# Layer 0's source factors by way of memory, with smaller layer 0 steps, in a two-layer graph attention kernel

## The chip, the cores and the metric

The kernel runs on one core of one Trainium2 chip. The metric is the device time of one execution in microseconds; the median of three runs stands for the kernel. The lower the better.

## What is computed

Two graph layers run one after the other on 16 independent graphs ("blocks" of the batch) with 1024 nodes and 256 features each, all in float32. Cut to what matters here:

```python
# layer 0, four heads of 64 (the adjacency holds 0 or 1, so only edge type t = 0 occurs)
h = einsum('bnd,hde->bhne', x, W)
weight = e_src[:, :, :, None] + e_dst[:, :, None, :]     # h with a_src, h with a_dst
weight = leaky_relu(weight, 0.01)
weight = where(adj == 0, -1e9, weight)
out = relu(softmax(weight) @ h + bias) + h               # then a norm per head
x = layernorm(x + out)
...
# layer 1, eight heads of 32, queries = keys = values
normed = layer_norm(x)
scores = einsum('bhqd,bhkd->bhqk', qkv, qkv) * scale
attn = softmax(where(adj > 0, scores, -inf))
x = x + attn @ qkv
y = layer_norm(x)
x = layernorm(... + x + gelu(y @ W1 + b1) @ W2 + b2)
```

## The kernel before

**Layer 0's trick.** The exponential of the leaky rectifier of a sum is the larger of two products of factors. After a factor that cancels in the softmax, a weight is `max(source factor, destination factor) * mask`. The source factor is exp(0.99 e_src): one number for each node and head, wanted along the free dimension of a tile and equal on all 128 partitions. The destination factor `dinv` is one number for each partition. So one VectorE (DVE) instruction makes 128x512 weights: `p = max(cb, dinv) * mask` (`weights`, line 569), where `cb` holds the source factors of 512 nodes for two heads, spread over the partitions.

**How the source factors come about before.** `prepare` (line 481) goes through the eight groups of 128 nodes of a block, two at a time (`GB = 2`). For each it turns x and the adjacency on TensorE (`transpose_rows`, `turn_mask`), multiplies by `w0e` (264 columns: h, and the two logit terms), and ScalarE copies the four source logits of each node into `apart[g]`, 32 columns apart. `turn_sources` (line 538) transposes `apart` on TensorE and writes the exponential as rows into `esr`, a tile in on-chip memory, where head h lies at partition 32h. In `attention0` (line 551), `spread_factor` (line 558) spreads a row over the partitions: a matmul of a 32x128 matrix of ones in one row (`spread`) with 512 columns of `esr` for each of two heads, into two of the four PSUM banks `ps` that layer 1 uses as well, and two ScalarE copies into `cb`.

**Layer 0's attention.** 16 steps for each block: 2 halves of the queries (`n`), 4 heads, 2 parts of four key groups (`j4`). In a step TensorE does 32 matmuls (64 records, since a float32 matmul leaves two) of a 64-column tile each; in the profile they are `acc<-v,p`, a "bout" below. The weights of the next step are issued right after (`ps = weights(*steps[i + 1])`). After the last step of a head comes `residual0`; after every two heads `after0` (line 636) normalises, and after the fourth it also makes layer 1's input: normed, transposed into `nT`, with gains into `v1`.

**Layer 1.** `attention1` (line 720) has 32 steps a block: four logit matmuls of 32 rows each (`ps<-nT`, eight records) into four `ps` banks, four ScalarE exponentials of 128x512, two DVE mask products, and three steps later the products with the values (`po<-v,p`, `po<-p,v`, `po<-p,unit`). `mlp` (line 858) has 32 units of eight records (`ps<-yT,w_sb` with Gelu, and `po<-w_sb,hid`), and ends each group in `last_norm`, which stores the output by SyncE's queue (SP).

**What sets the order.** The program is unrolled. All instructions of TensorE (PE), ScalarE (ACT), DVE and GpSimd (POOL) stand in the order in which this Python code issues them. Layer 0 of block b+1 and layer 1 of block b are two generators; each `yield` gives a number of units of work and the things that the next part needs. The loop at line 1007 picks one at a time: layer 0 if its place (`done0 / WORK0`) is behind the course of `wanted()` (line 994), which rises with layer 1's place along `COURSE` (line 992), else layer 1; and the other one when the picked one's needs are later than the other's by more than 0.3 us in a model, within `SLACK`. The model is the class `Pace` (line 90): it holds for each engine when it is free, and for each tile when it was written and last read, from a cost for each instruction. Small chains (norms, transposes) are begun with `begin` and run by `advance` when the model says that they are ready. SP's DMA issues are not in that hand order.

```python
WORK0 = NB // GB * 3.25 + 2.0 + NB * H0 // 2 * 2.0
ATTN1 = 2.0 + 2.5 * (NH * NB * H1 // QUAD)
WORK1 = ATTN1 + NB // GB * (1.75 * FC / 2 + 3.5 * GB)
SLACK = 0.06
COURSE = [(0.0, 1.0), (ATTN1, 1.42), (WORK1 - 10.0, 2.0), (WORK1, 2.0)]
```

With the kernel's sizes WORK0 is 47, ATTN1 is 82 and WORK1 is 138: layer 0 of the next block is to be 42% done when layer 1's attention ends, and done ten units before the MLP's end. All helper calls go through one line, so the profile gives L61 for nearly everything; groups are told apart by their tiles.

Of the kernel before, what the change touches and what calls it, by code (L numbers as in the profile page):

```python
# [39 lines left out]
P = 128  # L40
# [49 lines left out]
class Pace:  # L90
# [20 lines left out]
    def through(self, tile):  # L111
        return max(self.written.get(tile, 0.0), self.read.get(tile, 0.0))

    def now(self):
        return self.free["tensor"]
# [55 lines left out]
def fast_path(  # L171
# [37 lines left out]
    Q = 32  # L209
    TILE = 64  # L210
    PAIR = 2
    GB = 2
# [12 lines left out]
    ]  # L225
    small = ring("small", 3)
    ps_s = ring("ps_s", 4, space=PSUM)
    ps_a = ring("ps_a", 1, space=PSUM)
# [10 lines left out]
    nc.vector.tensor_copy(identb, ident)  # L239

    spread = const.tile([P, P], F32, name="spread")
    nc.vector.memset(spread, 0.0)
    for h in range(H0):
        nc.vector.memset(spread[h * Q : h * Q + 1, :], 1.0)

# [18 lines left out]
    for c in range(DC):  # L264
        for h in range(H0):
            nc.scalar.dma_start(w0e[:, c, h * HO : (h + 1) * HO], w0[h, c * P : (c + 1) * P, :])

    apart = [const.tile([P, H0, Q], F32, name=f"apart{g}") for g in range(GB)]
    for t in apart:
        nc.vector.memset(t, 0.0)  # L270
    terms = ((a_src, nc.sync, w0e[:, :, D + H0 : D + 2 * H0]), (a_dst, nc.scalar, w0e[:, :, D : D + H0]))
# [208 lines left out]

    def prepare(b, hb, esr, v0, dinv, mask):

# [17 lines left out]

        turning, scaling = [], []
        for k in range(0, NB, GB):
            i = b * (NB // GB) + k // GB
            load_blocks(i + 1)
            xk = x_blocks.pop(i)
            xT = one.tile([P, DC, GB * P], F32, name="xT")
            transpose_rows(xT, xk)
            yield 0.45, bank0_ready
            turn_mask(k)
            yield 0.5, bank0_ready, xT  # L510
            if k % BPH == 0:

                finish_norms(b - 1, k // BPH)
                hb.append(one.tile([P, BPH, D], F32, name=f"hb{k // BPH}"))
            for g in range(GB):
                if g == 0:

                    for chain in turning:
                        complete(chain)
                ph, _ = bank0([P, D + 2 * H0])  # L520
                for c in range(DC):
                    nc.tensor.matmul(ph, xT[:, c, g * P : (g + 1) * P], w0e[:, c, :], start=c == 0, stop=c == DC - 1)
                nc.scalar.copy(apart[g][:, :, 0], ph[:, D + H0 : D + 2 * H0])
                nc.scalar.activation(v0[:, k + g, :, HO], ph[:, D : D + H0], AF.Exp)
                nc.scalar.activation(dinv[:, k + g, :], ph[:, D : D + H0], AF.Exp, scale=-0.99)
                scaling.append(values0(v0[:, k + g, :, :], ph))
                begin(scaling[-1], "vector", ph)
                nc.scalar.copy(hb[-1][:, (k + g) % BPH, :], ph[:, 0:D])
                yield 0.9, bank0_ready
                if g == 0:  # L530
                    turn_mask(k + 1)
                    yield 0.5, bank0_ready, xT
            turning.append(turn_sources(esr[:, k * P : (k + GB) * P]))
            begin(turning[-1], "tensor", bank0_ready, *apart)
        for chain in turning + scaling:
            complete(chain)

    def turn_sources(dst):
        es, _ = bank0([P, GB, P])
        for g in range(GB):  # L540
            nc.tensor.transpose(es[:, g, :], apart[g].rearrange("p h q -> p (h q)"), ident)
        nc.scalar.activation(dst, es.rearrange("p g q -> p (g q)"), AF.Exp, scale=0.99)
        yield from ()

# [5 lines left out]

    def attention0(b, hb, v0, esr, dinv, factors, mask, rinv):

        groups = [(n, pair) for n in range(NH) for pair in range(H0 // PAIR)]
        steps = [(n, hd, j4) for n in range(NH) for hd in range(H0) for j4 in range(0, NB, 4)]

        def spread_factor(n, pair):

            cb = two.tile([P, PAIR, HALF], F32, name="cb")  # L560
            pbs = [ps_s.tile([P, HALF], F32, name="ps") for _ in range(PAIR)]
            for e in range(PAIR):
                q = slice((pair * PAIR + e) * Q, (pair * PAIR + e + 1) * Q)
                nc.tensor.matmul(pbs[e], spread[q, :], esr[q, n * HALF : (n + 1) * HALF], start=True, stop=True)
            for e in range(PAIR):
                nc.scalar.copy(cb[:, e, :], pbs[e])
            return cb

        def weights(n, hd, j4):
            ps = []  # L570
            cb = cbs[n, hd // PAIR]
            for j2 in (j4, j4 + 2):
                p = four.tile([P, 2, HALF], F32, name="p0")
                for i in range(2):
                    nc.vector.scalar_tensor_tensor(
                        p[:, i, :],
                        cb[:, hd % PAIR, :],
                        dinv[:, j2 + i, hd : hd + 1],
                        mask[n][:, j2 + i, :],
                        op0=OP.max,  # L580
                        op1=OP.mult,
                    )
                ps.append(p)
            return ps

        def products(ps, hd, j4, av):
            for i in range(4):
                for q in range(BPH):
                    for at in range(0, P, TILE):
                        nc.tensor.matmul(  # L590
                            av[at : at + TILE, q, :],
                            ps[i // 2][:, i % 2, q * P + at : q * P + at + TILE],
                            v0[:, j4 + i, hd, :],
                            start=j4 + i == 0 and q == 0,
                            stop=j4 + i == NB - 1 and q == BPH - 1,
                        )

        cbs = {groups[0]: spread_factor(*groups[0])}
        yield 1.0,
        nc.vector.tensor_copy(factors, v0[:, :, :, HO])  # L600
        ps = weights(*steps[0])
        yield 1.0, bank0_ready, *ps
        for i, (n, hd, j4) in enumerate(steps):
            if j4 == 0:
                av, bank = bank0([P, BPH, HO + 1])
                bank["busy"] = True
            products(ps, hd, j4, av)
            advance()
            if i + 1 < len(steps):
                ps = weights(*steps[i + 1])  # L610
            if j4 == 0 and i + 3 < len(steps) and hd % PAIR == PAIR - 1:
                g = steps[i + 3][0], steps[i + 3][1] // PAIR
                cbs[g] = spread_factor(*g)
            if j4 == NB - 4:
                h = hb[n][:, :, hd * HO : (hd + 1) * HO]
# [5 lines left out]
                if hd % PAIR == PAIR - 1:  # L621
                    norms[b, n, hd] = after0(b, n, hd, hb[n])
                    begin(norms[b, n, hd], "vector", done(residual), hb[n])
            yield (2.0, *ps, *([bank0_ready] if j4 == NB - 4 else []))

# [94 lines left out]
    def attention1(half, mask, rinv, half_done):  # L720
# [8 lines left out]
        def exponentials(n, quad, jb):  # L729
            keys = slice(jb % BPH * P, (jb % BPH + 1) * P)  # L730
            of_keys, of_queries = half(jb // BPH)[2], half(n)[2]
            tiles = [ps_s.tile([P, HALF], F32, name="ps") for _ in range(QUAD)]
            for e in range(QUAD):
                q = slice(e * HD, (e + 1) * HD)
                nc.tensor.matmul(tiles[e], of_keys[q, quad, keys], of_queries[q, quad, :], start=True, stop=True)
            ps = []
            for e in range(0, QUAD, PAIR):
                p = eight.tile([P, PAIR, HALF], F32, name="p")
                for i in range(PAIR):
                    nc.scalar.activation(p[:, i, :], tiles[e + i], AF.Exp, scale=SCALE1)  # L740
                ps.append(p)
            return ps
# [198 lines left out]
    def layer0():  # L941
        for b in range(B):
# [5 lines left out]
            hb = []  # L948
            esr = one.tile([P, N], F32, name="esr")
            dinv = two.tile([P, NB, H0], F32, name="dinv")  # L950
            v0 = one.tile([P, NB, H0, HO + 1], F32, name="v0")
            mask = [two.tile([P, NB, HALF], U8, name=f"mask{n}") for n in range(NH)]
            yield from prepare(b, hb, esr, v0, dinv, mask)
            handed[b] = seen, rinv1, mask
            yield from attention0(b, hb, v0, esr, dinv, factors, mask, rinv0)
        place[0][:] = B, 0.0
# [30 lines left out]

    WORK0 = NB // GB * 3.25 + 2.0 + NB * H0 // 2 * 2.0
    ATTN1 = 2.0 + 2.5 * (NH * NB * H1 // QUAD)
    WORK1 = ATTN1 + NB // GB * (1.75 * FC / 2 + 3.5 * GB)  # L990
    SLACK = 0.06
    COURSE = [(0.0, 1.0), (ATTN1, 1.42), (WORK1 - 10.0, 2.0), (WORK1, 2.0)]

# [477 lines left out]
```

## Time and profile before

| what | value |
|---|---|
| median of 3 runs | 3573.72 us (3570.82 to 3583.27) |
| the profiled execution | 3564.78 us |
| its span, first to last instruction | 3563.0 us |
| PE matmul busy | 3443.4 us, 97% |
| DVE busy | 2989.8 us, 84% |
| ACT busy | 2010.2 us, 56% |
| mean granted TensorE clock | 0.983 |
| DMA | 97.51 MB in 77809 packets |

Times in the profile are microseconds from the first instruction, if not marked ns. A group's row gives the tiles as out<-in, the shapes, the count, then busy time, the mean ns of one, and the engine's idle time just before these instructions with what ended it. Matmul ends are modelled and matmuls overlap, so the distance from the start of one run of matmuls to the start of the next says more than their length: a matmul that waits may count as busy.

### The profile page before, as it was taken

How to read it: one execution, taken by the hardware profiler on the slowest of the kernel's cores; microseconds unless marked ns; L12 is line 12 of the kernel's file. 1: busy time of each engine (PE TensorE's matmuls, PEld its weight loads, DVE VectorE, ACT ScalarE, POOL GpSimd, SP SyncE). 2: the span in 40 equal slices, each digit the busy share in tenths (PEclk: the TensorE clock that was granted, in tenths of full speed). 3: DMA queues.
4: the chain of work that ended last, by engine and by line, in shares of the span. 5: the costliest groups of instructions: out<-in, count | busy, mean ns of one | idle time of the engine just before them, and what ended most of it. 6: DMA issues, size and time to landing. Idle time of an engine off the chain costs nothing.

```text
span 3563.0 us, 141472 instructions
## 1 busy us (share of the span) xinstructions
PE 3443.4 (97%) x64417; PEld 2329.2 (65%) x64417; DVE 2989.8 (84%) x5267; ACT 2010.2 (56%) x4320; POOL 413.7 (12%) x424
## 2 busy tenths in 40 slices
PE   6799999999999999999999999999999999999998
PEld 4458576675856658576585766757567585765846
DVE  5888898988888888898888979888798888988883
ACT  2564746547375563845647466474654737556373
POOL 0102011010110101011020110101101011010100
PEclk9899999999999999999999999999999999999999
DMA  4111101011020110201111010110201102010000
GB/s 107 32 20 34 30 14 41 12 34 30 16 45 9 37 24 17 47 12 35 21 30 33 13 39 15 34 30 14 41 13 33 30 16 45 9 37 9 16 6 14
DMA packets 77809, 97.51 MB, mean 27 GB/s; under 512 B 9104, under 2 KB 60048, under 8 KB 77200
## 3 DMA queue, kind: packets, MB, share of 16 engines
q0 software_dynamic: 18432, 33.56, 6.4%
q1 hardware_dynamic: 57184, 53.76, 5.0%
q8 instruction: 506, 8.29, 1.0%
q10 hardware_dynamic: 1584, 1.05, 0.1%
q14 instruction: 103, 0.84, 0.1%
HBM read 105.13 MB, written 16.78 MB: 34 GB/s over the span
## 4 chain that ended last, share of the span: by engine, by line
PE 91%; ACT 5%; DVE 2%; issue 1%; DMA 0%; POOL 0%; ACTq 0%; POOLq 0%; DVEq 0%
PE po L61 36%; PE ps L61 34%; PE acc L61 21%; ACT p L61 2%; DVE p L61 1%; ACT sq L61 1%; ACT mask L61 1%; ACT xT L61 0%; ACT z L61 0%; DMA w0e<-in_L_gnn_W_dram 0%; DVE hb L61 0%; ACT cb L61 0%; ACT hb L61 0%; POOL r L61 0%; DVE z L61 0%
## 5 line engine op out<-in xcount | busy, mean ns | idle before, releaser
L61 ACT ACTIVATE p<-ps 128x512 f32<-128x512 f32 x2048 | 1061.0, 616 | 417.3 <-PE ps L61 417.3
L61 DVE TENSOR_TENSOR p<-p,mask 128x1024 f32<-128x1024 f32 x1024 | 1188.9, 1217 | 27.0 <-ACT p L61 26.8
L61 PE MATMUL ps<-nT 32*128 32x512 f32 x4096 | 794.6, 651 | 12.3 <-ACT cb L61 9.8
L61 DVE SCALAR_TENSOR_TENSOR p<-cb,dinv,mask 128x512 f32<-128x512 f32 x1024 | 698.9, 743 | 23.3 <-ACT cb L61 23.3
L61 PEld LDWEIGHTS po<-v,p 128*32 128x32 f32 x32768 | 398.6, 110 | 317.0 <-issue 264.8
L61 ACT ACTIVATE hid<-ps,b_sb 128x256 f32<-128x256 f32 x512 | 242.5, 474 | 639.6 <-PE ps L61 639.6
L61 PE MATMUL acc<-v,p 128*64 128x65 f32 x16384 | 547.6, 225 | 18.3 <-DVE p L61 16.3
L61 PEld LDWEIGHTS acc<-v,p 128*64 128x64 f32 x16384 | 507.9, 139 | 83.6 <-issue 38.8
L61 PE MATMUL po<-p,v 128*32 128x512 f32 x2048 | 553.5, 615 | 0.0
L61 PE MATMUL po<-p,unit 128*32 128x512 f32 x2048 | 553.1, 615 | 0.0
L61 PE MATMUL ps<-yT,w_sb 128*128 128x256 f32 x2048 | 478.4, 383 | 0.0
L61 PE MATMUL po<-w_sb,hid 128*128 128x256 f32 x2048 | 474.6, 384 | 0.0
L61 PEld LDWEIGHTS po<-w_sb,hid 128*128 128x128 f32 x2048 | 381.7, 190 | 64.8 <-issue 11.4
L61 PEld LDWEIGHTS ps<-yT,w_sb 128*128 128x128 f32 x2048 | 380.3, 190 | 62.9 <-issue 11.4
L61 PEld LDWEIGHTS ps<-nT 32*128 32x128 f32 x4096 | 286.2, 186 | 166.2 <-ACT p L61 56.8
L61 PE MATMUL po<-v,p 128*32 128x33 f32 x32768 | 390.5, 198 | 4.4 <-issue 4.4
L61 PEld LDWEIGHTS po<-p,v 128*32 128x32 f32 x2048 | 78.7, 109 | 340.0 <-issue 210.8
L61 POOL TENSOR_TENSOR r<-v,mhalf 128x1 f32<-128x1 f32 (+1 forms) x192 | 152.8, 801 | 842.0 <-DVE v L61 493.0
L61 DVE TENSOR_TENSOR z<-acc,bias_r 128x256 f32<-128x256 f32 x128 | 54.1, 423 | 200.0 <-ACT hb L61 200.0
L61 POOL TENSOR_TENSOR r<-v1s,mhalf 128x4 f32<-128x4 f32 x32 | 61.7, 1927 | 1092.9 <-DVE v1s L61 1092.9
L61 POOL DMA_DIRECT2D ak<-in_adj_dram x128 | 69.7, 545 | 976.9 <-PE acc L61 963.1
L61 PE MATMUL acc<-w0e,xT 128*128 128x264 f32 x512 | 149.3, 415 | 20.0 <-issue 10.4
(109 smaller groups left out, 2909.4 us busy)
## 6 DMA issues: line engine op xcount, KB each, us to landing
ak<-in_adj_dram POOLq DMA_DIRECT2D x128, 256.0 KB, 3.9
xk<-in_x_dram SPq DMA_DIRECT2D x64, 256.0 KB, 2.8
xl<-in_x_dram SPq DMA_DIRECT2D x32, 512.0 KB, 3.9
out_dram<-z SPq DMA_DIRECT2D x128, 128.0 KB, 1.7
w_sb<-in_L_gnn_W_dram SPq DMA_DIRECT2D x2, 1024.0 KB, 6.7
v<-in_L_gnn_a_src_dram SPq DMA_DIRECT2D x2, 320.0 KB, 4.4
v<-in_L_gnn_a_dst_dram ACTq DMA_DIRECT2D x1, 320.0 KB, 6.5
xl<-in_L_gnn_a_dst_dram ACTq DMA_DIRECT2D x1, 320.0 KB, 7.8
```

The lines of the kernel that those rows point to most:

```text
L61: return method(*args, **kwargs)
```

## The change

There are four parts.

1. The source factors are no longer turned on TensorE. ScalarE writes exp(0.99 e_src) straight from the PSUM bank into a small tile `es` (128 nodes by four heads). A transfer on SP stores each `es[:, g, :]` with its two dimensions exchanged into `esr`, now a tile of four rows by 1024 in the chip's large memory with two buffers. `spread_factor` is now one transfer on SP, which reads two rows of 512 and writes them to all 128 partitions of `cb` (source stride 0 over partitions). The tiles `spread` and `apart`, `turn_sources`, the spreading matmuls and the copies to `cb` are gone. The first two `cb` of a block are loaded when half of `prepare` is done; the others at key group 2 of the second head of a pair, two pairs ahead.
2. A step of layer 0's attention has two key groups instead of four (32 steps of one unit instead of 16 of two units), and weights are issued three steps ahead (`AHEAD = 3`).
3. `Pace.together`: the model takes the four logit banks of a layer 1 step as free together, when the last one is, and as written together.
4. The course: 1.38 instead of 1.42, and layer 0 done 14 units before the MLP's end instead of ten. WORK0 keeps its value.

```diff
+    def together(self, tiles):
+        names = [t.tensor.name for t in tiles]
+        for times in (self.read, self.written):
+            times.update(dict.fromkeys(names, max(times.get(name, 0.0) for name in names)))
...
+    AHEAD = 3
...
+    memory = ctx.enter_context(tc.tile_pool(name="memory", bufs=2, space=bass.MemoryType.DRAM))
...
-                    for chain in turning:
-                        complete(chain)
...
-                nc.scalar.copy(apart[g][:, :, 0], ph[:, D + H0 : D + 2 * H0])
+                if g == 0:
+                    es = small.tile([P, GB, H0], F32, name="es")
+                nc.scalar.activation(es[:, g, :], ph[:, D + H0 : D + 2 * H0], AF.Exp, scale=0.99)
...
-            turning.append(turn_sources(esr[:, k * P : (k + GB) * P]))
-            begin(turning[-1], "tensor", bank0_ready, *apart)
-        for chain in turning + scaling:
+            for g in range(GB):
+                at = (k + g) * P
+                nc.sync.dma_start(esr[:, at : at + P].rearrange("h p -> p h"), es[:, g, :])
+            if k + GB == BPH:
+                for at in ((0, 0), (0, 1)):
+                    cbs[at] = spread_factor(esr, *at)
+        for chain in scaling:
             complete(chain)
-
-    def turn_sources(dst):
-        es, _ = bank0([P, GB, P])
-        for g in range(GB):
-            nc.tensor.transpose(es[:, g, :], apart[g].rearrange("p h q -> p (h q)"), ident)
-        nc.scalar.activation(dst, es.rearrange("p g q -> p (g q)"), AF.Exp, scale=0.99)
-        yield from ()
...
+    def spread_factor(esr, n, pair):
+        cb = two.tile([P, PAIR, HALF], F32, name="cb")
+        rows = esr[pair * PAIR : (pair + 1) * PAIR, n * HALF : (n + 1) * HALF]
+        nc.sync.dma_start(cb, bass.AP(tensor=rows.tensor, offset=rows.offset, ap=[[0, P], [N, PAIR], [1, HALF]]))
+        return cb
...
-        steps = [(n, hd, j4) for n in range(NH) for hd in range(H0) for j4 in range(0, NB, 4)]
-
-        def spread_factor(n, pair):
-
-            cb = two.tile([P, PAIR, HALF], F32, name="cb")
-            pbs = [ps_s.tile([P, HALF], F32, name="ps") for _ in range(PAIR)]
-            for e in range(PAIR):
-                q = slice((pair * PAIR + e) * Q, (pair * PAIR + e + 1) * Q)
-                nc.tensor.matmul(pbs[e], spread[q, :], esr[q, n * HALF : (n + 1) * HALF], start=True, stop=True)
-            for e in range(PAIR):
-                nc.scalar.copy(cb[:, e, :], pbs[e])
-            return cb
+        steps = [(n, hd, j) for n in range(NH) for hd in range(H0) for j in range(0, NB, PAIR)]
...
-        cbs = {groups[0]: spread_factor(*groups[0])}
-        yield 1.0,
         nc.vector.tensor_copy(factors, v0[:, :, :, HO])
-        ps = weights(*steps[0])
-        yield 1.0, bank0_ready, *ps
-        for i, (n, hd, j4) in enumerate(steps):
+
+        ps = [weights(*step) for step in steps[:AHEAD]]
+        yield 1.0, bank0_ready, ps[0]
+        for i, (n, hd, j) in enumerate(steps):
...
-            products(ps, hd, j4, av)
+            products(ps.pop(0), hd, j, av)
             advance()
-            if i + 1 < len(steps):
-                ps = weights(*steps[i + 1])
-            if j4 == 0 and i + 3 < len(steps) and hd % PAIR == PAIR - 1:
-                g = steps[i + 3][0], steps[i + 3][1] // PAIR
-                cbs[g] = spread_factor(*g)
-            if j4 == NB - 4:
+            if i + AHEAD < len(steps):
+                ps.append(weights(*steps[i + AHEAD]))
+            if j == NB - PAIR * AHEAD and hd % PAIR == PAIR - 1 and (n, hd // PAIR) in groups[:-2]:
+
+                at = groups[groups.index((n, hd // PAIR)) + 2]
+                cbs[at] = spread_factor(esr, *at)
+            if j == NB - PAIR:
...
-            yield (2.0, *ps, *([bank0_ready] if j4 == NB - 4 else []))
+            yield (1.0, *ps[:1], *([bank0_ready] if j == NB - PAIR else []))
...
+            nc.together(tiles)
             for e in range(QUAD):
                 q = slice(e * HD, (e + 1) * HD)
                 nc.tensor.matmul(tiles[e], of_keys[q, quad, keys], of_queries[q, quad, :], start=True, stop=True)
+            nc.together(tiles)
...
-    COURSE = [(0.0, 1.0), (ATTN1, 1.42), (WORK1 - 10.0, 2.0), (WORK1, 2.0)]
+    COURSE = [(0.0, 1.0), (ATTN1, 1.38), (WORK1 - 14.0, 2.0), (WORK1, 2.0)]
```

## The prediction, made before the changed kernel was run

> **What bounds the kernel now.** I read the page first (busy time, chain), then the groups of instructions, then windows of one middle block, then TensorE's timeline.
>
> ```profile
> PE 3443.4 (97%) x64417; PEld 2329.2 (65%) x64417; DVE 2989.8 (84%) x5267; ACT 2010.2 (56%) x4320; POOL 413.7 (12%) x424
> PE 91%; ACT 5%; DVE 2%; issue 1%; DMA 0%; POOL 0%; ACTq 0%; POOLq 0%; DVEq 0%
> ```
>
> TensorE (PE) is busy 97% of the span and carries 91% of the chain that ended last: a PE microsecond taken away counts, unless a wait behind it takes its place. Blocks repeat every 217 to 218 us. I split one in two: layer 1's MLP (with most of layer 0's attention between) and layer 1's attention (with layer 0's preparation of the next block).
>
> ```profile
> core 0: us, PE busy (x) PEld busy (x) DVE busy (x) ACT busy (x) POOL busy (x), PEclk, DMA share, GB/s
> 1341.00:1425.00 84.00, 84.00 (x992) 71.77 (x992) 72.03 (x159) 30.46 (x61) 16.93 (x14) 1.00 0.06 17
> 1425.00:1559.60 134.60, 131.17 (x3041) 73.34 (x3041) 114.14 (x169) 95.08 (x209) 8.87 (x12) 0.97 0.17 32
> ```
>
> The MLP stage, 84.0 us, is dense on PE (84.00 busy, clock 1.00), DVE at 86%. The attention stage, 134.6 us, looks as busy, but there a waiting matmul stretches: in the timeline eight logit records `ps<-nT` need 1.07 us from start to next start, and many take 1.70 to 3.3.
>
> The rows the change removes:
>
> ```profile
> L61 PE MATMUL ps<-esr,spread 32*128 32x512 f32 x256 | 72.1, 640 | 0.0
> L61 ACT COPY cb<-ps 128x512 f32<-128x512 f32 x128 | 68.7, 589 | 152.0 <-PE ps L61 152.0
> L61 PE MATMUL acc<-ident,apart 128*128 128x128 f32 x128 | 25.5, 280 | 0.2 <-ACT apart L61 0.2
> L61 ACT ACTIVATE esr<-acc 128x256 f32<-128x256 f32 x64 | 25.2, 394 | 0.0
> L61 ACT COPY apart<-acc 128x4 f32<-128x4 f32 x128 | 24.0, 188 | 50.5 <-PE acc L61 50.5
> ```
>
> [...] So each new store is 512 four-byte pieces, and the row load queues behind it; no store of this shape is in the trace. [...]
>
> **The change, per block of 217 us.** TensorE's timeline, MLP stage (start, length; I take start to next start):
>
> ```profile
> 1382.10 2.09 PE L61 MATMUL acc<-v,p 128*64 128x65 f32 x64
> 1384.12 1.13 PE L61 MATMUL ps<-esr,spread 32*128 32x512 f32 x4
> 1385.17 1.13 PE L61 MATMUL po<-w_sb,hid 128*128 128x256 f32 x4
> ```
>
> 1. *Spread matmuls, MLP stage:* 1385.17 − 1384.12 = 1.06 us, twice a block: −2.1.
> 2. *Spread matmuls, attention stage:*
>
> ```profile
> 1512.62 0.38 PE L61 MATMUL acc<-ident,apart 128*128 128x128 f32 x2
> 1512.93 1.13 PE L61 MATMUL ps<-esr,spread 32*128 32x512 f32 x4
> 1513.89 2.44 PE L61 MATMUL ps<-nT 32*128 32x512 f32 x8
> ```
>
> One pair costs 0.96 (1513.89 − 1512.93); a second (1538.89) runs beside logits. −1.0. Behind them the logits need 2.37 and 3.34 (1538.89 to 1542.22) instead of 1.07: they share the four `ps` banks and ScalarE must first copy `cb` out. That is 3.6 us of stall. Some returns as the ordinary 1.70 form (0.63 each); bounds 1.8 and 3.6, I take −2.7.
>
> 3. *Source transposes:* 1512.93 − 1512.62 = 0.31, four a block: −1.2.
> 4. *ScalarE in the attention stage:* off go 8 × 0.19 (`apart`), 4 × 0.39 (`esr`), 4 × 0.59 (`cb`) = 5.4; on come 8 exponentials of 128x4 at the 0.21 of the `v<-acc` row = 1.7. ScalarE is 95 of 134.6 us busy, so most is off the path: bounds 0 and −2, I take −0.7.
> 5. *Transfers:* 8 stores of 2 KB, 4 loads of 512 KB a block, all on SP. Nearest for the store: the 1024-element `b_sb` load, 2.2 us to landing; `g_c` 6.0 is the upper end. Nearest for the load: `xl`, 512 KB, 3.9. Chained, 6 to 10 us. The first two rows are loaded half-way through the preparation, tens of us early; a later one is issued eight half-steps before its first use (about 26 us at 3.3 us for half-step and MLP unit). I take 0; upper bound +1. Queued behind on SP: `xk` loads, which two buffers keep a block pair ahead, and output stores, 1.7 us with three `z` buffers. The store waits for ScalarE's exponential, the row load for DVE's last read of its buffer: SP may stand some us, covered by the same buffers. Without that cover DVE would stop at `z`, the stall itself being the price. DVE's wait on `cb` (23.3 us, 16 times) goes, but in blocks with layer 1 beside it PE has other work: 0.
> 6. *Layer 0 parts of two blocks.* Now 64 records take 2.02. Counting records in 1363.90 to 1364.40 and to 1365.00 (24, 44) gives 0.030 us a record, 1.9 for 64: starting a bout costs 0.10 to 0.15. MLP records before a same-mode transpose take 0.87 for four (1388.73 to 1389.60), 3.48 for 16; between two bouts 16 take 3.65 (1393.44 to 1397.10): 0.17 for entering and leaving. So 0.27 to 0.32 per bout, I take 0.30. The MLP stage had 11 bouts, about one per two MLP units. With half-units and a course rising (2.0 − 1.38)/42 × 1.75 × 47 = 1.2 half-steps per MLP unit, nearly every unit is followed by one: some 27 half-steps in 23 bouts. 12 more × 0.30 = +3.6; bounds 7 × 0.27 = +1.9 (many doubled) and 16 × 0.32 = +5.1.
> 7. *Course 1.42 to 1.38:* about five half-steps move from attention into the MLP. They cost 0.03 × 32 = 0.96 there and free slightly less where they filled stalls, while smaller pieces fill more of them: bounds −0.5 and +1.2, I take +0.5.
> 8. *Layer 0 ends four units earlier (−14):*
>
> ```profile
> 1425.00:1447.00 22.00, 20.29 (x221) 10.58 (x220) 17.42 (x42) 17.64 (x42) 3.72 (x5) 0.84 0.30 73
> ```
>
> The attention stage starts with ScalarE at 17.64 of 22 us, because the last norm and its transposes of layer 0 fall there, and PE at clock 0.84 (22 × 0.16 = 3.5 us lost). Four earlier units could move that into the MLP; the first logits, without products beside them, stay bound by exponentials. Bounds 0 and −4, I take −1.0.
>
> 9. *Logits together in the model:* no instruction changes, the order sees the wait for four banks. Bounds 0 and −3, I take −0.8.
>
> Sum: −2.1 − 1.0 − 2.7 − 1.2 − 0.7 + 3.6 + 0.5 − 1.0 − 0.8 = −5.4 us. Fifteen blocks of layer 0 run beside layer 1: −81. Block 0 runs alone and waits for DVE; losing transpose and `cb` at its start gives about −1 (DVE waited 0.67 on `cb` there). Together −82. The profiled execution took 3564.8 (span 3563.0 and 1.8 around it): 3483. The median of the runs is 3573.7, 9 higher: **3492**.
>
> **Rivals.**
> - *The start of attention empties* (8 and 4 in full): −10 a block, 3573.7 − 150 = 3424. For it: ScalarE's load and the clock there. Against: four units are 7 us, and the norm's chain ends in forced steps anyway.
> - *Switches eat the gain:* every half-step its own bout (+5.1), only 1.0 of item 2's stall saved, nothing from 4, 8, 9: −2.1 − 1.0 − 1.0 − 1.2 + 5.1 + 0.5 = +0.3, about 3575. For it: the half-units. Against: the stall behind `cb` is plain.
> - *Slower: DVE becomes what the MLP stage waits for.* Layer 0's share there rises from 1.04 to 1.2 half-steps per MLP unit. DVE: 72 us less 44 × 0.68 (698.9 us busy over 1024 on the `p<-cb,dinv,mask` row) leaves 42 of other work; over 24 dense units 1.75, plus 1.2 × 1.37 = 3.4. PE: 1.74 + 1.2 × 0.96 + 0.30 = 3.2. From an average wait of 5.4/24 = 0.22 us per half-step it is slower; at 0.35 it costs 8.4, so +3.0 a block and 3619. Against: 42 spreads over the whole stage, and weights run three half-steps ahead.
> - *The transfers don't do it:* a row later than 26 us. Against: 6 to 10 us. Counted with the last.
>
> **Chances.** Forecast 0.63, its own range 3440 to 3555; empty start 0.17; eaten 0.08; DVE or late rows 0.12. Range 3410 to 3578: it leaves out the lower third of the empty start (0.06), the slower case (0.12) and an edge of the eaten one (0.02). What a measurement can tell is about 0.3%, 11 us: faster 0.80, same 0.08, slower 0.12.
>
> **What would show it.** No `spread` or `apart` rows; `ps<-nT` total below 794.6; about 23 MLP bouts of 32 records at 1.1 us; MLP stage some 87 us, attention stage some 125; PE busy down by some 80. Wrong if DVE's `p` ends PE's waits in the MLP stage, if bouts stay paired, or if DVE waits for a `cb` transfer.

## The result and the profile after

The changed kernel is slower by a quarter: median 4461.36 us of 4 runs (4444.25 to 4478.3) against 3575.71 us of 4 runs of the kernel before (3570.82 to 3583.27), a ratio of **1.2483 [1.2442, 1.2524]**. The forecast was 3492. The profiled execution took 4444.25 us, with a span of 4442.5, 879.5 above the 3563.0 of before. One run of a kernel below (rows_course) took 4648.44 us at a granted clock of 0.629, against 0.97 in its other three, and is left out of its figures.

The page's first lines and its chain, after:

```profile
span 4442.5 us, 140860 instructions
PE 3592.3 (81%) x64033; PEld 2364.6 (53%) x64033; DVE 2986.4 (67%) x5260; ACT 1920.9 (43%) x4128; POOL 431.5 (10%) x424
PE 74%; issue 17%; ACT 6%; DVE 2%; DMA 1%; another core or an unknown queue 0%; POOL 0%; ACTq 0%; POOLq 0%; DVEq 0%
```

The instructions went as planned: 384 matmuls fewer, DVE the same, ScalarE 89 us less. Yet TensorE carries 74% of the chain instead of 91%, and 17% of it, some 755 us, is "issue": an engine that waits for nothing that the profile shows. Next, the same two stages of a middle block as before, in the after profile's windows:

```profile
core 0: us, PE busy (x) PEld busy (x) DVE busy (x) ACT busy (x) POOL busy (x), PEclk, DMA share, GB/s
1705.10:1793.90 88.80, 88.80 (x1122) 75.45 (x1116) 75.97 (x169) 28.70 (x59) 18.13 (x14) 1.00 0.08 25
1793.90:1980.00 186.10, 136.83 (x2795) 71.12 (x2797) 109.72 (x158) 91.50 (x199) 8.82 (x12) 0.81 0.29 30
```

The MLP stage (84.0 before) is 88.8 us and full, near the 87 of the forecast. The attention stage went from 134.6 to 186.1 with fewer instructions on TensorE, DVE and ScalarE. TensorE stands for 49 us of it (186.10 − 136.83; before 3.4), and its clock fell from 0.97 to 0.81. Eight stores of `es` fall into this stage. One of them in the after profile's timeline (lines of other engines and runs left out):

```profile
243.72 16.85 SPq L61 DMA_DIRECT2D esr<-es  x2
...
244.93 4.62 DVE L61 TENSOR_TENSOR p<-p,mask 128x1024 f32<-128x1024 f32 x4
...
246.97 0.53 POOL L61 DMA_DIRECT2D ak<-in_adj_dram  x1 [7.56 <-PE acc L61]
...
248.62 0.61 PE L61 MATMUL po<-v,p 128*32 128x33 f32 x48
257.43 0.48 PE L61 MATMUL po<-v,p 128*32 128x33 f32 x16 [8.19 <-issue]
257.84 2.13 PE L61 MATMUL acc<-w0e,xT 128*128 128x264 f32 x4
```

A run of 64 equal products breaks off after 48. TensorE stands 8.19 us, waiting for nothing that the profile shows ("issue"), and goes on with the other 16, which read tiles of the same names. DVE had finished its last mask product (244.93 + 4.62) 7.9 us before TensorE went on. TensorE resumes 13.7 us after SP began on the first of the two stores. The waits of the whole profile (us in total, times, longest) put most of it at these products:

```profile
PEld po L61 <- issue: 1219.2, 1334, 11.7
PE po L61 <- issue: 672.5, 157, 11.5
```

Before, they were:

```profile
PEld po L61 <- issue: 487.7, 1166, 1.5
PE po L61 <- issue: 4.4, 8, 0.9
```

And what the forecast feared of the transfers did not come: DVE waited 3.5 us for `cb` in all, in the row of its weights:

```profile
L61 DVE SCALAR_TENSOR_TENSOR p<-cb,dinv,mask 128x512 f32<-128x512 f32 x1024 | 709.7, 743 | 3.5 <-DMA cb<-esr 3.5
```

### The profile page after: what moved, and what is told of

Read it like the earlier page. It is cut to its first block, busy times and chain, and to the rows that moved or that the text cites. A ratio compares the mean times of both kernels' runs of the same rounds, so it can differ in the third digit from the quotient of the medians.

```text
span 4442.5 us, 140860 instructions
## 1 busy us (share of the span) xinstructions
PE 3592.3 (81%) x64033; PEld 2364.6 (53%) x64033; DVE 2986.4 (67%) x5260; ACT 1920.9 (43%) x4128; POOL 431.5 (10%) x424
## 3 DMA queue, kind: packets, MB, share of 16 engines
q0 software_dynamic: 18432, 33.56, 12.5%
q8 instruction: 503, 8.24, 1.0%
## 4 chain that ended last, share of the span: by engine, by line
PE 74%; issue 17%; ACT 6%; DVE 2%; DMA 1%; another core or an unknown queue 0%; POOL 0%; ACTq 0%; POOLq 0%; DVEq 0%
PE po L61 30%; PE ps L61 26%; PE acc L61 18%; ACT p L61 2%; DVE p L61 1%; ACT mask L61 1%; ACT sq L61 1%; ACT o L61 1%; DMA esr<-es 1%; ACT z L61 0%; DMA w0e<-in_L_gnn_W_dram 0%; ACT hb L61 0%; DMA cb<-esr 0%; ACT oT L61 0%; DVE hb L61 0%
## 5 line engine op out<-in xcount | busy, mean ns | idle before, releaser
L61 PEld LDWEIGHTS po<-v,p 128*32 128x32 f32 x32768 | 451.2, 117 | 1029.8 <-issue 979.4
L61 PE MATMUL po<-v,p 128*32 128x33 f32 x32768 | 460.2, 205 | 661.5 <-issue 660.8
L61 PE MATMUL ps<-nT 32*128 32x512 f32 x4096 | 776.0, 745 | 23.8 <-issue 22.0
L61 PE MATMUL po<-p,v 128*32 128x512 f32 x2048 | 600.5, 662 | 11.6 <-issue 11.6
L61 PE MATMUL po<-p,unit 128*32 128x512 f32 x2048 | 599.8, 662 | 0.0
L61 PE MATMUL acc<-v,p 128*64 128x65 f32 x16384 | 575.5, 226 | 25.2 <-DVE p L61 19.9
L61 PEld LDWEIGHTS ps<-nT 32*128 32x128 f32 x4096 | 250.7, 213 | 135.8 <-issue 75.6
L61 ACT ACTIVATE mask<-acc,shift_c 128x1024 uint8<-128x1024 bf16 x128 | 144.3, 1127 | 354.7 <-PE acc L61 275.6
L61 POOL TENSOR_TENSOR r<-v,mhalf 128x1 f32<-128x1 f32 (+1 forms) x192 | 171.3, 900 | 660.3 <-DVE v L61 574.7
L61 DVE RECIPROCAL ranges<-po 128x8 f32<-128x8 f32 x64 | 13.3, 208 | 288.6 <-PE po L61 288.6
```

The source lines that it names most:

```text
L61: return method(*args, **kwargs)
```

## Which part costs it: three runs

My theory was that the 128 stores, each of 512 four-byte pieces that lie side by side in memory, stop TensorE, and that nobody's waiting for their data matters. The rival was the half steps with the new order. (Beside the queue of the stores, the page of after has a queue of kind `instruction`, q8, with 503 packets of 16 KB; more on it below.) The times below stand beside runs of the kernel before on the same chip, 3578.79 us for these three.

**stores_beside**: the kernel before, with the stores of the change added; nothing reads `aside`. (This and the later kernels with `aside` compute what the kernel before does, and additionally the unread tile.)

```diff
+        aside = memory.tile([H0, N], F32, name="aside")
...
+                if g == 0:
+                    es = small.tile([P, GB, H0], F32, name="es")
+                nc.scalar.activation(es[:, g, :], ph[:, D + H0 : D + 2 * H0], AF.Exp, scale=0.99)
...
+            for g in range(GB):
+                at = (k + g) * P
+                nc.sync.dma_start(aside[:, at : at + P].rearrange("h p -> p h"), es[:, g, :])
```

> The kernel before, with the change's 128 stores (512 pieces of 4 bytes each) added from a tile of their own into memory that nothing reads; ScalarE also makes the 128 small exponentials. No instruction waits for the data. Theory A (the stores hold up other transfers, among them the fetching of TensorE's instructions, some 7 us each): 3576 + 128 x 6.9 = about 4460 us, TensorE idle with 'issue' some 800 us. Rival B (the new order of the work costs the time) and rival C (the row loads into cb, or what waits for them): 3576 to 3610 us.

Measured: 4530.24 us, 951 more than before, 7.4 us a store. The waits of this kernel look like those of after:

```profile
PEld po L61 <- issue: 1156.8, 1305, 10.5
PE po L61 <- issue: 599.4, 151, 10.4
```

The stores alone give the whole loss. Nothing waits for them.

**rest_alone**: the change without its first part. Source factors as before (TensorE and `cb` copies), with half steps, weights three ahead, `together` and the new course.

```diff
+    AHEAD = 3
...
-        steps = [(n, hd, j4) for n in range(NH) for hd in range(H0) for j4 in range(0, NB, 4)]
+        steps = [(n, hd, j) for n in range(NH) for hd in range(H0) for j in range(0, NB, PAIR)]
...
+            nc.together(tiles)
...
+    COURSE = [(0.0, 1.0), (ATTN1, 1.38), (WORK1 - 14.0, 2.0), (WORK1, 2.0)]
```

> The kernel before with its own way to the source factors (transpose, spreading matmul, copies), but with steps of two key groups, weights three steps ahead, logits together in the model and the new course. Theory A: 3576 plus what the prediction's items 6 to 9 give, +3.6 +0.5 -1.0 -0.8 = +2.3 us a block, about 3610 us (3540 to 3650). Rival B: over 4300 us. Rival C: like A.

Measured: 3568.91 us, 0.9974 [0.9962, 0.9985]. Parts 2 to 4 cost nothing here; on the old path they even save 9 us.

**rows_store**: the changed kernel, but the factors are turned on TensorE as before and stored as rows: four pieces of 1 KB for every two node groups. The loads that spread `cb` stay.

```diff
-                nc.sync.dma_start(esr[:, at : at + P].rearrange("h p -> p h"), es[:, g, :])
...
+        for g in range(GB):
+            nc.tensor.transpose(es[:, g, :], apart[g].rearrange("p h q -> p (h q)"), ident)
+        row = small.tile([P, GB * P], F32, name="row")
+        nc.scalar.activation(row, es.rearrange("p g q -> p (g q)"), AF.Exp, scale=0.99)
+        nc.sync.dma_start(dst, row[0:P:Q, :])
```

> The changed kernel, but the source factors are turned on TensorE as before and stored as four runs of 1 KB instead of 1024 pieces of 4 bytes for two blocks; the 64 row loads into cb, the half steps, the model and the course are the changed kernel's. Theory A: the stall goes, and what the prediction forecast remains less the transposes that stay (1.2 + 0.5 us a block): about 3518 us (3430 to 3580). Rival B and rival C: over 4300 us.

Measured: 3543.46 us, 0.9899 [0.9882, 0.9915]. Between after and this kernel lie 4442.5 − 3543.9 = 898.6 us of span, 7.0 for each of the 128 stores. The 64 loads of 512 KB, with source stride 0 over the partitions, are no problem: DVE's idle time before the weights that read `cb` is 0.0 us here. So it is the stores, and their shape.

## What in the shape: four runs

Each is stores_beside with another layout of `aside`; the payload is always 2 KB.

**stores_spaced**: each four-byte piece in a 512-byte stretch of its own.

```diff
-        aside = memory.tile([H0, N], F32, name="aside")
+        aside = memory.tile([H0, N, P], F32, name="aside")
...
-                nc.sync.dma_start(aside[:, at : at + P].rearrange("h p -> p h"), es[:, g, :])
+                nc.sync.dma_start(aside[:, at : at + P, 0].rearrange("h p -> p h"), es[:, g, :])
```

> As stores_beside, the same number of 4-byte pieces, but every piece goes to 512 bytes of its own in memory instead of beside its neighbour. If pieces that share a stretch of memory must be written one after the other (A1): near 3600 us. If each small piece costs by itself wherever it goes (A2): 4400 to 4500 us as in stores_beside. Rivals B and C: 3576 to 3610 us.

**stores_64b** and **stores_4perline**: the same with `[H0, N, 16]` (64 bytes apart) and `[H0, N, 4]` (16 bytes apart).

> As stores_spaced, but the pieces lie 64 bytes apart instead of 512. If it is 64-byte lines that are shared in stores_beside: near 3590 us as in stores_spaced. If the shared stretch is longer, up to 512 bytes: clearly over 3700 us.

> As stores_64b with the 4-byte pieces 16 bytes apart, so four of them to 64 bytes; 512 pieces a store. If the pieces of one 64-byte line are written one after the other, a store lands in about a quarter to a third of the 12 to 14 us, 3 to 5 us, [...]: 3580 to 3650 us. If touching pieces are what matters, 3585 us and 2.2 us to landing; if a longer stretch is shared, over 3900 us.

**stores_16b**: no exchange of dimensions; 128 adjacent pieces of 16 bytes.

```diff
+        aside = memory.tile([N, H0], F32, name="aside")
...
+                nc.sync.dma_start(aside[at : at + P, :], es[:, g, :])
```

> The kernel before with 128 unread stores of the same 2 KB, as 128 adjacent pieces of 16 bytes (four heads of a node side by side). A quarter of the pieces; if the pieces of one shared stretch are written one after the other, a quarter of stores_beside's loss or less [...]: 3580 to 3800 us. If any store under 512 bytes a piece costs a fixed time: 4400 us.

| store | time, us | before on that chip | a store costs |
|---|---|---|---|
| 4 B pieces side by side | 4530.24 | 3578.79 | 7.4 |
| 4 B pieces, 16 B apart | 3586.9 | 3575.3 | 0.09 |
| 4 B pieces, 64 B apart | 3585.47 | 3567.15 | 0.14 |
| 4 B pieces, 512 B apart | 3588.43 | 3578.79 | 0.08 |
| 16 B pieces side by side | 3583.97 | 3567.15 | 0.13 |

Each of these kernels was run once. The 10 to 18 us that the last four lie above the kernel before are no more than that kernel's own spread (3556.91 to 3578.0 in its seven runs around 3567.15). The number of pieces is the same 512 in the first four rows: stores_beside and stores_spaced both have 145396 packets, 76688 of them under 512 bytes. That is 528 a store more than before ((145396 − 77809) / 128); in stores_16b, with 128 pieces, it is 144, so each piece is a packet and 16 more come with a store. The line of the page of stores_spaced:

```profile
DMA packets 145396, 97.80 MB, mean 27 GB/s; under 512 B 76688, under 2 KB 127632, under 8 KB 144784
```

So neither the count of pieces nor their size costs anything that matters; what costs is four-byte pieces side by side (distances between 4 and 16 bytes were not tried). The profile's DMA view has the time to landing of the other stores (last column, median us). For stores_spaced:

```profile
aside<-es SPq DMA_DIRECT2D x128, 2.0 KB, 2.5
```

for stores_64b:

```profile
aside<-es SPq DMA_DIRECT2D x128, 2.0 KB, 2.2
```

and for stores_16b:

```profile
aside<-es SPq DMA_DIRECT2D x128, 2.0 KB, 2.1
```

That is what the prediction had taken for the store (2.2). For the two other shapes the view gives no time, but the trace has increments of the stores' semaphores. With pieces 16 bytes apart all 16 increments of a store are recorded, and the last comes 4.5 us after the issue (median of 128 stores). With adjacent pieces only some are recorded, five in the median. The last of these comes 13.7 us after the issue in stores_beside and 12.9 in after (medians over the stores with no other within 13 us), so these are lower bounds.

The time to landing thus rises from 2.2 us over 4.5 to some 13 as one, four or 16 four-byte pieces share 64 bytes. The 4.5 lie in the 3 to 5 us that were expected for pieces of the same 64 bytes written one after the other. That neighbours wait for each other fits, but is not shown: in stores_16b four pieces share 64 bytes as well, and they land in 2.1 us. Small pieces at a distance cost this kernel nothing that can be told from its spread; only four-byte pieces right beside each other do.

## Why TensorE stands: two runs

TensorE reads nothing that the stores write. So I looked at what else the stores hold up. The queue of the adjacency loads on the page of before (packets, MB, share of 16 engines):

```profile
q0 software_dynamic: 18432, 33.56, 6.4%
```

and this queue and that of instructions on the page of after:

```profile
q0 software_dynamic: 18432, 33.56, 12.5%
...
q8 instruction: 503, 8.24, 1.0%
```

The adjacency loads move the 33.56 MB of before in packets that take 2.4 times as long together (12.5% of 4442.5 us against 6.4% of 3563.0): the stores do slow transfers that have nothing to do with them. The start of every packet is in the trace. In stores_beside 90 stores have no other within 13 us. Nine in ten of these have begun all their 512 pieces within 2.6 us of the issue. Then, from 3 to 10 us after the issue, 5.8 packets a microsecond begin, of all queues together, against 32 in the mean of the run; after 52 of the 90 stores it is at most one packet in these 7 us. In after it is so behind 52 of 91. So it is not the taking in of the pieces that lasts: behind an adjacent store nearly all of the core's transfers stand still.

As to q8, 8.24 MB in 503 packets is 16 KB a packet; TensorE's 64033 matmuls and as many weight loads, divided by 503, are 255 instructions a packet. With TensorE's own waits and branches counted in (128373 records in after), the packets keep step with 256 of its instructions: 91% of them begin within one half of a cycle of 256 in after and 96% in before, against 52 to 55% with a cycle of 255 or 257. With the kind of the queue, `instruction`, it fits that these packets bring TensorE's instructions. A theory is then that TensorE runs out of instructions ("issue" is 1% of the chain before and 17% after). How many it has in hand no run shows; the stops counted below come after some 250.

To see whether a store starves TensorE, I wanted stores where it uses instructions more slowly: in the MLP stage 1984 matmuls and loads in 84.0 us (24 a microsecond), against 6082 in 134.6 us (45) in the attention stage: a little over half the rate.

**stores_mlp**: the kernel before, with the stores in the MLP and a constant tile as their source.

```diff
+                if f % 4 == 0:
+                    at = (n * BPH + q + f // 4) * P
+                    nc.sync.dma_start(aside[:, at : at + P].rearrange("h p -> p h"), unit[:, 0:H0])
```

> As stores_beside (128 unread stores of 512 adjacent 4-byte pieces, eight a block), but issued in layer 1's MLP, where TensorE works through its instructions at less than half the rate of the attention stage. If TensorE starves of instructions behind a store (A), what it has in hand lasts about twice as long there and most of a store's time is covered: under 3576 + 128 x 3.5 = 4020 us, near 3700 to 3950. If it waits for data that the store holds up, or is stopped by the store itself (D): about as in stores_beside, 4300 to 4530 us.

Measured: 3696.18 us against 3567.15. This run did not test what it was made for. Its source is ready from the start, so nothing holds SP back, and SP issued the stores in one go at the beginning, where they only delayed the x loads behind them. SP's timeline of stores_mlp:

```profile
74.21 164.74 SPq L61 DMA_DIRECT2D aside<-unit  x103
```

and its longest wait of TensorE, most of the loss of 129 us in one place:

```profile
PE acc L61 <- ACT sq L61: 101.9, 1, 101.9
```

The other blocks last 217.5 us as before. What it tells is only that a chain of such stores holds up what is queued behind it on SP, by some 1.6 us each (164.74 / 103).

**stores_mlp2**: as stores_mlp, but each stored tile is a copy that ScalarE makes there.

```diff
+                if f % 4 == 0:
+                    at = (n * BPH + q + f // 4) * P
+                    es = small.tile([P, H0], F32, name="es")
+                    nc.scalar.copy(es, hid[f // 4][:, f % 4, 0:H0])
+                    nc.sync.dma_start(aside[:, at : at + P].rearrange("h p -> p h"), es)
```

> The kernel before, with 128 stores of 512 adjacent four-byte pieces that nothing reads, eight in each block's layer-1 MLP. This time the stored tile is a copy that ScalarE makes of four columns of `hid` right there, so SP can't issue a store before its place. In the attention stage such a store cost 7.4 us (stores_beside). There TensorE works through some 45 matmuls and weight loads a microsecond (6082 in 134.6 us), in the MLP stage through 24 (1984 in 84.0). Theory A, TensorE runs out of instructions because the store holds up the engines that bring them: at half the rate the instructions in hand last longer, so a store costs half as much or less, 1 to 4 us: 3700 to 4080 us, with TensorE's idle time put down to issue. Theory B, the store stops TensorE for a time of its own, whatever it executes: 7 to 7.5 us each: 4460 to 4540. Theory C, the store hurts only where something of the attention stage (the adjacency load on POOL's queue, the x loads) waits beside it: under 3620.

Measured: 3921.13 us against 3583.5, a single run of each, 2.6 us a store: inside what theory A gave, far from the others. Two stores in this kernel's timeline, lines of TensorE's matmuls and of SP, and one of DVE:

```profile
1524.65 0.36 SPq L61 DMA_DIRECT2D aside<-es  x1
1525.55 2.09 PE L61 MATMUL acc<-v,p 128*64 128x65 f32 x64
...
1527.57 3.72 PE L61 MATMUL ps<-yT,w_sb 128*128 128x256 f32 x16
1531.19 0.55 SPq L61 DMA_DIRECT2D aside<-es  x1
1531.22 1.73 PE L61 MATMUL acc<-v,p 128*64 128x65 f32 x51
...
1532.52 2.73 DVE L61 SCALAR_TENSOR_TENSOR p<-cb,dinv,mask 128x512 f32<-128x512 f32 x4
...
1538.70 0.96 PE L61 MATMUL acc<-v,p 128*64 128x65 f32 x13 [5.75 <-issue]
```

After the first store TensorE works on for more than 8 us, through a bout, 16 slow records and most of another bout, then it breaks off after 51 records of 64. DVE does not: three of its four `p` start while TensorE stands.

Counted in the trace, for stores with no other within 13 us, is what TensorE executed between the store's issue and the longest stop that begins in the 16 us behind it:

| kernel | such stores | with a stop over 2 us | instructions until the stop, median (10% to 90%) | issue of the store to resumption, us, median |
|---|---|---|---|---|
| stores_beside | 90 | 88 | 248 (204 to 332) | 12.2 |
| after | 91 | 91 | 253 (211 to 297) | 11.4 |
| stores_mlp2 | 15 | 3 | 248 to 256 (all three) | 14.9 to 16.1 (all three) |

In the attention stage TensorE executes some 250 instructions in the 5.4 to 5.5 us (medians) behind the issue, stops, and goes on when the store is about landed. Behind the last store of each MLP in stores_mlp2 the same 250 instructions need 13 us, and by then little of the store is left. In twelve of the fifteen cases TensorE doesn't stop for 2 us. In three it stands 2.1 to 3.2 us, from 12.8 us or later, which the profile puts down to ScalarE's exponentials. So a store costs TensorE about the time that is left until it lands when some 250 instructions have gone by. That much the runs show.

That TensorE comes to the end of the last packet's instructions is not shown, and two things in the trace speak against it in this plain form. First, it would then always stop at the same place of the 256. Counted from the program's start in stores_beside, 92% of q8's packets begin within one half of the 256 instructions; of the 88 stops no half holds more than 51 (in after, 55 of 91). Second, a packet of q8 takes 1.48 us in the mean in after (1.08 before; the longest 9.8), and in 85 of the 88 stops in stores_beside none is under way in the last microsecond before TensorE goes on. Whether TensorE waits for instructions whose packet is already over, or for something else that goes with each of its instructions (the profiler's own records, say), no run tells: none without the profiler is on record. A halt of the whole core it is not, as DVE's line above shows. What it is that holds TensorE stays open.

## The other terms of the sum: four runs

With the stores out of the way, the rest of the forecast can be checked. Their kernel before ran at 3567.15 us for the first, 3575.3 for the others.

**rows_only**: the kernel before with rows_store's path for the factors, and old steps, old model and old course: items 1 and 2 alone.

> The kernel before with the source factors by way of memory in 1 KB rows as in rows_store, but with steps of four key groups, the old model and the old course. The prediction's items 1 and 2 alone (-2.1 -1.0 -2.7 = -5.8 us a block) would give 3576 - 87 = 3489 us. From the two runs at hand (rest_alone 0.9974, rows_store 0.9899 of before) the parts add up if this is 0.9925, 3552 us: then items 1 and 2 were two to three times too large.

Measured: 3493.6 us, **0.9783 [0.975, 0.9816]**. The logit row shows where: 766.0 us, with the spread records and the stall behind them gone (794.6 before):

```profile
L61 PE MATMUL ps<-nT 32*128 32x512 f32 x4096 | 766.0, 660 | 1.5 <-ACT p L61 1.3
```

**hops**: rows_only without the transposes: items 3 and 4 as well. The factors go to memory in 16-byte pieces, each half comes back as four rows, goes out again as rows of 2 KB, and is spread from there.

```diff
+                nc.sync.dma_start(nodes[(k + g) * P : (k + g + 1) * P, :], es[:, g, :])
...
+                row = one.tile([H0, HALF], F32, name="row")
+                nc.sync.dma_start(row, nodes[half, :].rearrange("n h -> h n"))
+                nc.sync.dma_start(esr[:, half], row)
```

> rows_only without any transpose of the sources on TensorE: es is stored as 16-byte pieces, a half of the nodes is read back as four rows in 4-byte pieces into on-chip memory, and these rows are stored as 2 KB runs, from which cb is loaded. Items 3 and 4 of the prediction (-1.2 and up to -0.7 us a block): 20 to 28 us under rows_only, a ratio near 0.972. If small pieces are dear in reading too, or the SP queue holds up the others: over 1.00.

Measured: 3476.24 us, **0.9716 [0.9694, 0.9738]**. It is the fastest of all, beats both kernels, and gives what the change's first part was meant to give. Reading four-byte pieces does no harm that can be seen here; DVE's wait for `cb` is 14.6 us in all:

```profile
L61 DVE SCALAR_TENSOR_TENSOR p<-cb,dinv,mask 128x512 f32<-128x512 f32 x1024 | 698.7, 743 | 14.6 <-DMA cb<-esr 14.6
```

**rows_half**: rows_only with half steps and weights three ahead (item 6), old model and course. **rows_course**: rows_only with `together` and the new course (items 7 to 9), old steps.

> rows_only with layer 0 steps of two key groups and weights three steps ahead, old model and old course. The prediction's item 6 (twelve more bouts at 0.30 us, +3.6 us a block) on fifteen blocks: 54 us over rows_only, a ratio to before near 0.993. If the half steps cost nothing and the course does: 0.978 like rows_only.

> rows_only with the logits taken together in the model and the new course, steps of four key groups. The prediction's items 7 to 9 (+0.5 -1.0 -0.8 = -1.3 us a block): 20 us under rows_only, a ratio near 0.973. If it is the course that loses what rows_store lost against rows_only: near 0.990.

Measured: rows_half 3594.29 us, 1.0059 [1.0037, 1.0081]; rows_course 3536.05 us (median of three), 0.9899 [0.9875, 0.9923]. Both are slower than rows_only, and both expectations were off: by the ratios the edits alone cost 1.0059 / 0.9783 = 1.028 and 0.9899 / 0.9783 = 1.012, or 99 and 41 us, each within some 14, where 54 and −20 had been forecast. The two together (rows_store, 0.9899) cost 41 as well, not 140. In rows_course DVE has a larger part of the chain, 26% (2% in rows_only):

```profile
PE 63%; DVE 26%; ACT 6%; issue 3%; POOL 0%; DMA 0%; ACTq 0%; POOLq 0%; DVEq 0%
```

Its largest wait of TensorE shows where; it comes once a block, more than 100 us into the attention stage, and rows_only does not have it:

```profile
PE po L61 <- DVE ranges L61: 42.7, 15, 2.9
```

The stages over the middle blocks (us), from TensorE's timeline: the MLP stage from the first `ps<-yT` to the next block's first `ps<-nT`, the attention stage from there to the next `ps<-yT`:

| kernel | block | MLP stage | attention stage | bouts and half-steps in the MLP |
|---|---|---|---|---|
| before | 217.1 | 83.6 | 133.6 | 11, 22 |
| rows_only | 212.8 | 81.4 | 131.3 | 11, 22 |
| hops | 210.9 | 81.4 | 129.5 | 11, 22 |
| rows_half | 219.0 | 90.8 | 128.2 | 23, 25 |
| rows_course | 213.9 | 87.9 | 126.0 | 13, 26 |
| rows_store | 215.3 | 88.8 | 126.5 | 19, 26 |
| after | 274.8 | 88.8 | 186 | 19, 26 |

## Why the prediction was wrong

**The step that failed is item 5, "Transfers", with its rival "The transfers don't do it".** It asked when a transfer lands and who waits for its data, and priced the store at the nearest load, 2.2 to 6.0 us, hidden by tens of microseconds; "I take 0; upper bound +1". The store took some 13 us to land, and even that would have been hidden: DVE waited 3.5 us for `cb` in the whole run. What the step left out is what happens meanwhile to work that doesn't need the data: other transfers nearly stand still, and TensorE stops some 250 instructions after the issue. That the store does this is shown (stores_beside); by which path it stops TensorE is not. In place of +1 stands the difference of the attention stages of after and rows_store, 186 − 126.5 = 59.5 us a block, or 7.4 for each of its eight stores. A load had been taken as a bound for a store of a shape that no row of the profile had; the bound was of the wrong kind, so the range was as well.

**Items 1 and 2** (−5.8 us a block with the stall): the mechanism was right; rows_only shows 217.1 − 212.8 = −4.3. The MLP stage fell by 2.2 (forecast 2.1), the attention stage by 2.3 (forecast 3.7). With 1.0 for the spreads there, 1.3 are left for the stall behind `cb`: half of the 2.7 taken, and under its lower bound of 1.8. **Items 3 and 4** (−1.9): right, −1.9 from rows_only to hops.

**Item 6** (+3.6): bouts and their price held, but the size of the step failed: +6.2 a block and 99 us in all against 54. The MLP stage grew by 9.4. From start to next start over ten blocks, its bouts take 4.6 more (three more half-steps among them, some 3.0), its MLP records 2.4 more; without the half-steps that is 4.0 for twelve more bouts, 0.33 each. The last 2.4 are twenty more records of other work, mainly layer 0's next preparation, which had moved into the MLP stage. The attention stage, though it has lost both, gave back only 3.1. **Items 7 to 9** (−1.3): the sign was wrong; +1.1 a block. In rows_course the MLP stage grew by 6.5, of which 5.1 are its bouts with four more half-steps, and the attention stage gave back 5.3. The MLP stage doesn't wait for DVE there, as the rival "DVE becomes what the MLP stage waits for" had it: TensorE waits 4.2 us in it in the whole run. DVE's part of the chain comes with waits in the attention stage, 42.7 us for `ranges` alone, 2.8 a block. Besides, the attention of the last block, with no layer 0 beside it, takes 118.4 us in place of 110.7. **6 to 9 together**: +2.3 forecast, +2.5 measured (rows_store against rows_only). That agreement is two errors that cancel: the parts don't add, and on the old path (rest_alone) the same edits save 9 us. Why they cancel was not settled.

Of what was to show each step: in after `spread` and `apart` are gone, the MLP stage is 88.8 (forecast 87), the half-steps in it are 26 (27), the bouts 19 (23). The attention stage would have been 126.5 (forecast 125), and PE's busy time in rows_store is 3356.2, 87 lower (forecast 80). With rows_store's stores in place of its own the changed kernel takes 3543.46 us, a per cent less than before and inside the range of the forecast; with the old steps and course as well, and the factors turned by memory as in hops, 3476.24.

## What to carry to other kernels

Ask of a new transfer not only who waits for its data, but what else uses the DMA engines while it runs, and don't take a load as the price of a store of another shape. Don't store a transposed tile to memory as adjacent four-byte pieces (7.4 us a store here); put four-byte pieces at least 16 bytes apart (0.09), store pieces of 16 bytes (0.13), store rows after turning them on TensorE (rows_only, 0.9783 of before), or turn them on the way back by reading (hops, 0.9716). When an engine idles with "issue" in the middle of a run of equal instructions, look at the DMA issues of the 12 us before, whoever's they are (TensorE went on a median of 11.4 and 12.2 us after the store's issue).

## What the hardware showed unasked

- 512 adjacent four-byte pieces written to memory take some 13 us to land (12.9 and 13.7, lower bounds); the same pieces 16 bytes apart, 4.5; 64 or 512 bytes apart, 2.2 to 2.5; the same 2 KB in 128 pieces of 16 bytes, 2.1.
- From 3 to 10 us after such an adjacent store at most one packet of any queue begins in more than half of the cases (52 of 90 in stores_beside).
- Where TensorE stops behind one, it stands for a median of 6.3 us (stores_beside) and 5.7 (after), and the clock of the stage is lower: 0.81 in place of 0.97 in the attention stage of after.
- In hops 32 loads of 2048 four-byte pieces, 16 bytes apart in memory, cost nothing that can be seen: with 3476.24 us it is the fastest kernel, and DVE waits 14.6 us for `cb` in all.
- A store whose source is ready is issued as soon as SP gets to it, however far its place in the program is: in stores_mlp 103 within 165 us, though eight belong to each block of 217 us. What is queued behind them waits.
